# A graph network's second and third layers: sums and splits from GpSimd to VectorE, forms and bias made one group earlier, PSUM pools kept open

## The chip, the cores and the metric

The kernel runs on one core of a Trainium2 chip. The metric is the device time of one execution in microseconds (us). Engines are named as in the profile: PE is TensorE (PEld its weight loads), DVE is VectorE, ACT is ScalarE, POOL is GpSimd, SP is SyncE, which here only issues DMAs.

## The reference

There are 2500 nodes with 256 features and 80000 edges, sorted by destination. After a layer norm with relu come three edge convolutions, and at the end a product with the concatenation of all four states:

```
def _edge_conv(x, src, dst, W, b):
    xi = x[dst]
    xj = x[src]
    m = jnp.concatenate([xi, xj - xi], axis=-1) @ W + b
    s = jax.ops.segment_sum(m, dst, num_segments=N)
    cnt = jax.ops.segment_sum(jnp.ones((dst.shape[0],), m.dtype), dst, num_segments=N)
    return s / jnp.maximum(cnt, 1.0)[:, None]
...
for W, b in ((W0, b0), (W1, b1), (W2, b2)):
    h = jax.nn.relu(_edge_conv(h, src, dst, W, b))
    xs.append(h)
cat = jnp.concatenate(xs, axis=-1)
return cat @ Wf + bf          # out = x + this, with h = relu(layernorm(x)) as input
```

## The kernel before

**What it computes.** The edges become a matrix of counts (how often node n is a source of node m), so a layer is `hT = relu(z summed by counts + hT times (Wa - Wb))` with `z = h Wb / count`. Destinations are cut into five groups of 504, 504, 504, 504 and 486 columns; sources into 20 tiles of 128 nodes, taken two at a time: a *pair of tiles*, number `q` from 0 to 9. `hT` holds the state transposed; `acc` gathers the output.

**Precision by parts.** TensorE's one-pass type fp32r keeps fewer bits than fp32, so every operand is cut in parts. `zh` and `zl` are high and low part of z. `Split(q)` makes three parts of the state of pair q: high (ACT), low (a subtraction), across (one more operation on DVE). `Forms` makes three matching parts of a weight block [Wb | Wf]: high, scaled and last on ACT, two lows and two acrosses on DVE. With both, `times` makes a product from 6 one-pass matmuls per tile; `times_whole` makes it from 2 fp32 matmuls, each of which TensorE runs in two passes (the profile counts both).

**Stages.**

- *Layer 0* builds the counts, group by group: DVE compares keys, PE adds, ACT copies; `finish` writes them to DRAM in bf16 (`a_dram`). `layer(0, g)` multiplies group g meanwhile. During the last group (g = 4) no counts are left to build.
- *Node stage* of layers 1 and 2, for each pair q in `orders[l]`: `Nodes.multiply` (12 one-pass matmuls of 512 columns), `parts` (ACT scales and copies into `tmp` and `zh`, DVE makes `zl` and adds to `acc` twice), `combine` (three subtractions and sums of z into `tmp`), `split` of the pair two places on, `sums` (ACT `sh`, DVE `sl`). Between them `Alone` multiplies the fifth group (8 matmuls of 486 columns per pair); `lone.end` adds its own product and ACT writes `hT`.
- *Stream stage*: groups 0 to 3 are done as two 2x2 block products by a scheme of seven products. There are 2 x 5 chunks; a chunk has seven blocks of counts, cast from bf16 in `staged` to fp32r in `block` (seven buffers, pool `ready`), and each block is used by 4 matmuls of 504 columns. Three blocks are casts on ACT (`b11`, `b21`, `b22`), four are sums on DVE (`r1` to `r4`). `Stream.make` stays five blocks ahead. `tick(n)` puts small jobs between the 70 steps, the splits and forms of the next layer among them.
- *Last layer*: for each pair 12 one-pass matmuls of 256 columns, two additions to `acc`, two output DMAs; splits up to three pairs ahead.

**What sets the order.** Each engine runs its instructions in the order of the Python code (`InOrder` keeps it). Semaphores and the sizes of the pools make them wait. `banks(n, alone)` closes a PSUM pool and opens another; the first tile of a new pool waits for the last users of all tiles of the closed one.

```
def split(q, V=POOLo):
    sp = splits[q] = Split(q)
    sp.high()
    sp.low(V)
    sp.across(DVEo)
...
n.multiply(None if i < whole else splits.pop(q), forms, flat(l))
n.parts()
n.combine(POOLo)
```

All instructions recorded through `InOrder` stand under line L282 in the profile, so one goes by the tiles' names.

Of the kernel before, what the change touches and what calls it, by code (L numbers as in the profile page):

```python
# [313 lines left out]
def by_windows(ctx: ExitStack, tc: tile.TileContext, x, src, dst, Ws, bs, Wf, bf, out, missing):  # L314
# [3 lines left out]
    P = 128  # L318
# [597 lines left out]
    apools.append(first_layer.enter_context(tc.tile_pool(name="apool1", bufs=1)))  # L916
# [8 lines left out]


    LATE = [NT] * 4
    extra = chain(degrees(0), finish(0, a), later_loads(), degrees(1))
    for g in range(NG):
        at = {}  # L930
        own = LATE
        if g + 1 < NG:
            a1 = new_a(g + 1)
            one = build(g + 1, a1)
            left = -(-len([b for b in windows if b[0] == g + 1]) // TURN)
            units = NT + DC * DC
            at = {(i + 1) * (units - 1) // left - 1 for i in range(left)}
            if g:
                own = [u + 1 - i for i, u in enumerate(sorted(at)[1:5])]
        else:  # L940
            extra = shares()
# [19 lines left out]
    banks_of = ctx.enter_context(ExitStack())  # L961

    def banks(n, alone=0):
        nonlocal banks_of
        banks_of.close()
        banks_of = ctx.enter_context(ExitStack())
        ps.append(banks_of.enter_context(tc.tile_pool(name="ps_n", bufs=n, space=PSUM)))
        return banks_of.enter_context(tc.tile_pool(name="ps_alone", bufs=alone, space=PSUM)) if alone else None
# [3 lines left out]
    ready = ctx.enter_context(tc.tile_pool(name="ready", bufs=7))  # L972
# [14 lines left out]
    def combine(to, x, V):  # L987
        V.tensor_sub(to[:, M3:S5 + 1, :], x[:, 1::2, :], x[:, 0:2, :])
        V.tensor_sub(to[:, S2, :], to[:, M3, :], x[:, 3, :])
        V.tensor_add(to[:, M4, :], to[:, S2, :], x[:, 2, :])  # L990
# [3 lines left out]

    E12 = 4096.0
    C1 = 1.0 + 1.0 / E12
    DOWN = 1.0 - 0.5 / E12  # L1000

    class Split:

        def __init__(self, q):
            self.q = q
            t = stage.tile([P, 4 * GS], F32R, name="staged")
            self.parts = [t[:, k * 2 * D:(k + 1) * 2 * D].rearrange("p (c n) -> p c n", c=DC) for k in range(3)]
            self.h = hT[:, :, 2 * q * P:(2 * q + 2) * P]

        def high(self):  # L1010
            ACTo.activation(self.parts[0], self.h, AF.Copy, scale=DOWN)

        def low(self, V):
            V.tensor_sub(self.parts[1], self.h, self.parts[0].bitcast(F32))

        def across(self, V):
            V.scalar_tensor_tensor(self.parts[2], self.parts[1].bitcast(F32), -E12, self.parts[0].bitcast(F32),
                                   op0=OP.mult, op1=OP.add)

    class Forms:  # L1020

        def __init__(self, raw, n, V, rest):
            self.raw, self.n, self.V = raw, n, V
            self.rest = rest
            self.parts = [ready.tile([P, 2, 512], F32R, name="block")[:, :, :n] for _ in range(3)]

        def high(self):
            ACTo.activation(self.parts[0], self.raw, AF.Copy, scale=C1 * DOWN)

        def low(self):  # L1030
            for c in range(DC):
                self.V.scalar_tensor_tensor(self.rest[c], self.raw[:, c, :], C1, self.parts[0][:, c, :].bitcast(F32),
                                            op0=OP.mult, op1=OP.subtract)

        def scaled(self):
            for c in range(DC):
                ACTo.activation(self.parts[1][:, c, :], self.rest[c], AF.Copy, scale=E12)

        def across(self):
            for c in range(DC):  # L1040
                self.V.scalar_tensor_tensor(self.rest[c], self.parts[0][:, c, :].bitcast(F32), -1.0 / E12, self.rest[c],
                                            op0=OP.mult, op1=OP.add)

        def last(self):
            for c in range(DC):
                ACTo.activation(self.parts[2][:, c, :], self.rest[c], AF.Copy, scale=1.0 / C1)

# [5 lines left out]

    def times_whole(to, t, raw):
        for c in range(DC):
            PEo.matmul(to, hT[:, c, t * P:(t + 1) * P], raw[:, c, :], start=(c == 0), stop=(c == DC - 1))
# [4 lines left out]
    class Nodes:  # L1061
# [4 lines left out]
        def multiply(self, split, forms, raw):  # L1066
            self.banks = [bank(), bank()]
            for i, t in enumerate(self.two):
                if split is None:
                    times_whole(self.banks[i], t, raw)  # L1070
                else:
                    times(self.banks[i], split, i, forms)
# [17 lines left out]
        def combine(self, V):  # L1090
            self.raw = tmp()
            combine(self.raw.rearrange("p (s n) -> p s n", s=4), self.zf.rearrange("p (s n) -> p s n", s=4), V)
# [10 lines left out]
    class Pair:  # L1103
# [12 lines left out]
        def make(self, c, what, st, made):  # L1116
            to = made[what] = ready.tile([P, 2, 512], F32R, name="block")[:, :, :GS]
# [27 lines left out]
        def multiply(self, c, part, what, made):  # L1145
            if c == 0:
                self.bank[what] = bank()[:, :GS]
# [40 lines left out]
    class Alone:  # L1188

        def __init__(self, l, order, pool):  # L1190
            self.l, self.order = l, order
            self.c0, self.n = group_of(alone)
            self.to = [pool.tile([P, 512], F32, name="bank")[:, :self.n] for _ in range(DC)]
            self.blocks = {}

        def make(self, p):
            q = self.order[p]
            to = self.blocks[p] = ready.tile([P, 2, 512], F32R, name="block")
# [67 lines left out]
    DVEo.tensor_sub(ws[1][0], ws[1][0], ws[1][1])  # L1266
# [3 lines left out]
    splits = {}  # L1270
    forms = None

    def split(q, V=POOLo):
        sp = splits[q] = Split(q)
        sp.high()
        sp.low(V)
        sp.across(DVEo)

    def flat(l):
        return raws[l].rearrange("p c t d -> p c (t d)") if l < L else wfs[l]  # L1280

    for l in range(1, L):
        order = orders[l]
        whole = 2 if l == 1 else 0
        lone = Alone(l, order, banks(6, 2))
        if l == 1:
            load_alone(0, order)
            split(order[whole])
            forms = Forms(flat(l), 512, DVEo, [tmp(), tmp()])
            forms.high()  # L1290
            forms.low()
            forms.scaled()
            forms.across()
            forms.last()
        pending = []
        stream = Stream(l)
        for i in range(Q + LAG):
            if 0 < i <= Q:
                lone.make(i - 1)
            if i < Q:  # L1300
                q = order[i]
                n = Nodes(l, q)
                n.multiply(None if i < whole else splits.pop(q), forms, flat(l))
# [3 lines left out]
                n.combine(POOLo)  # L1307
# [12 lines left out]
        banks(8)  # L1320
# [6 lines left out]
        coming = []  # L1327

        def tick(n):
            if l == 1 and 2 <= n < 18 and n % 4 == 2:  # L1330
                part = acc[:, (n - 2) // 4 * 5:(n + 2) // 4 * 5, :]
                POOLo.tensor_add(part, part, bf_sb.unsqueeze(1).to_broadcast([P, 5, D]))
            if n == 3:
                combine(wsum, ws[l][0].rearrange("p c (o n) -> p (c o) n", o=2), DVEo)
# [4 lines left out]
            if n == 63:  # L1339
                if l + 1 < L:  # L1340
                    load_alone(0, after)
                else:
                    split(after[3])
            if n == 65:
                split(after[2])
            if n == 64:
                raw = flat(l + 1)
                coming.append(Forms(raw, 512 if l + 1 < L else D, DVEo, [raw[:, c, :] for c in range(DC)]))
                coming[0].high()
                coming[0].low()  # L1350
            if n == 66:
                coming[0].scaled()
# [5 lines left out]
        forms = coming[0]  # L1358

    order = orders[L]  # L1360
    for i, q in enumerate(order):
        po, sp = bank(), splits.pop(q)
        for k in range(2):
            times(po[:, k * D:(k + 1) * D], sp, k, forms)
# [46 lines left out]
```

## Time and profile before

| what | value |
|---|---|
| runs | 495.49, 497.53, 498.29 us; median 497.53 |
| profiled execution: own time | 495.88 us |
| profiled execution: span | 494.0 us |
| granted TensorE clock, mean | 0.99 |
| layer 0 / node 1 / stream 1 | 0-206 / 206-259 / 259-344 us |
| node 2 / stream 2 / last layer | 344-394 / 394-471 / 471-494 us |

The times of all rows are from the start of the span; the own time is 1.9 us longer than the span. In the rows, "x12" merges 12 like instructions, the second number of a timeline row is its length in us, and a bracket at its end says how long the engine was idle before it and what ended that. A matmul's row is longer than the distance to the next one (they overlap), so costs of matmuls are taken from start to start.

### The profile page before, as it was taken

To read this page: it belongs to the slowest core of one execution; us is meant where nothing else is said; L and a number is where in the kernel's file an instruction comes from. 1 tells how busy PE (TensorE), PEld (TensorE's weight loads), DVE (VectorE), ACT (ScalarE), POOL (GpSimd) and SP (SyncE) were. 2 spreads that over 40 slices of the span, in tenths; PEclk is the share of its full clock that TensorE was granted. 3 is DMA by queue.
4 is the path that set the end of the run, shared out by engine and by line. 5 is a ranking of instruction groups with operands and counts; after the bars stand their busy time and mean duration, and the time that the engine had idled before them with its cause. 6 is when DMAs were issued, how large, how long until landed. Compare 5 with 4: busy or idle time off the path is not lost.

```text
span 494.0 us, 7493 instructions
## 1 busy us (share of the span) xinstructions
PE 474.3 (96%) x2728; PEld 367.5 (74%) x2728; DVE 391.7 (79%) x743; ACT 264.6 (54%) x488; POOL 142.9 (29%) x158
## 2 busy tenths in 40 slices
PE   8999999999999999989996999999999999999994
PEld 4888888777777778558865877866788688687684
DVE  8999988888888850168689877997677769689885
ACT  5676677653734340298762444635787644365240
POOL 3682006100101010178786000111787200011252
PEclk9999999999999999999997999999999999999998
DMA  9310098970914509211392541210213944320024
GB/s 285 108 43 1 2 204 152 203 147 0 189 23 92 119 14 197 84 44 42 88 355 72 187 153 49 85 43 0 85 42 101 340 169 137 115 85 1 0 75 141
DMA packets 21847, 52.75 MB, mean 107 GB/s; under 512 B 1977, under 2 KB 12170, under 8 KB 21770
## 3 DMA queue, kind: packets, MB, share of 16 engines
q1 hardware_dynamic: 15018, 34.57, 20.9%
q0 software_dynamic: 5856, 16.51, 17.5%
q10 hardware_dynamic: 928, 1.11, 0.7%
q8 instruction: 23, 0.38, 0.3%
q14 instruction: 22, 0.18, 0.1%
HBM read 36.72 MB, written 16.10 MB: 107 GB/s over the span
## 4 chain that ended last, share of the span: by engine, by line
PE 64%; issue 13%; DVE 11%; POOL 6%; ACT 3%; DMA 2%; SPq 0%; DVEq 0%; POOLq 0%; ACTq 0%
PE bank L282 60%; DVE block L282 5%; PE pz L282 3%; POOL staged L282 2%; POOL acc L282 2%; DMA acc<-in_x_dram 1%; DVE staged L282 1%; DVE tmp L282 1%; POOL tmp L282 1%; DMA staged<-a_dram 1%; DVE st L282 1%; ACT hT L282 1%; POOL ed L282 1%; POOL es L282 0%; ACT block L282 0%
## 5 line engine op out<-in xcount | busy, mean ns | idle before, releaser
L282 ACT CAST block<-staged 128x1008 fp32r<-128x1008 bf16 x80 | 79.3, 1031 | 44.2 <-issue 42.8
L282 POOL TENSOR_TENSOR staged<-hT,staged 128x512 fp32r<-128x512 f32 x28 | 39.9, 1434 | 167.8 <-ACT staged L282 167.8
L282 PE MATMUL bank<-block,zh 128*128 128x504 f32 (+1 forms) x200 | 83.4, 417 | 2.4 <-ACT hT L282 1.3
L282 ACT CAST a<-bank 128x480 fp32r<-128x480 f32 (+1 forms) x105 | 52.9, 565 | 59.3 <-PE bank L282 59.2
L282 PE MATMUL bank<-a,zh 128*128 128x504 f32 (+1 forms) x200 | 84.3, 421 | 0.0
L282 DVE TENSOR_TENSOR one_m<-iota_m,key_m 128x1024 bf16<-128x1024 bf16 (+1 forms) x105 | 72.0, 686 | 14.1 <-PE bank L282 14.0
L282 PE MATMUL bank<-block,zl 128*128 128x504 f32 (+1 forms) x200 | 78.1, 391 | 0.0
L282 PE MATMUL bank<-a,zl 128*128 128x504 f32 (+1 forms) x200 | 77.8, 389 | 0.0
L282 PE MATMUL bank<-block,sh 128*128 128x504 f32 x160 | 69.9, 437 | 4.0 <-DVE block L282 4.0
L282 PE MATMUL bank<-block,staged 128*128 128x512 f32 (+1 forms) x336 | 69.8, 358 | 3.5 <-DVE staged L282 2.1
L282 DVE TENSOR_TENSOR one_n<-iota_n,key_n 128x480 bf16<-128x480 bf16 (+1 forms) x210 | 66.8, 359 | 0.0
L282 PEld LDWEIGHTS bank<-block,staged 128*128 128x128 f32 x336 | 55.1, 188 | 15.5 <-DVE staged L282 3.9
L282 PE MATMUL bank<-block,sl 128*128 128x504 f32 x160 | 63.0, 394 | 0.0
L282 POOL TENSOR_TENSOR tmp<-tmp 128x128 f32<-128x128 f32 (+1 forms) x60 | 46.0, 766 | 31.2 <-ACT tmp L282 24.7
L282 DVE SCALAR_TENSOR_TENSOR staged<-staged 128x512 fp32r<-128x512 f32 x28 | 22.6, 807 | 39.5 <-POOL staged L282 39.5
L282 DVE TENSOR_TENSOR block<-block,staged 128x1008 fp32r<-128x1008 f32 x40 | 52.5, 1313 | 1.4
L282 PEld LDWEIGHTS bank<-block,zh 128*128 128x128 f32 x200 | 38.1, 191 | 14.9 <-ACT hT L282 2.9
L282 POOL DMA_DIRECT2D a_dram<-a x20 | 10.7, 542 | 127.7 <-ACT a L282 127.4
L282 PEld LDWEIGHTS <-one_m 128*128 128x128 bf16 x834 | 39.1, 98 | 9.7 <-issue 3.2
L282 PEld LDWEIGHTS bank<-block,zl 128*128 128x128 f32 x200 | 38.2, 191 | 10.2 <-issue 2.8
L282 PEld LDWEIGHTS bank<-a,zh 128*128 128x128 f32 x200 | 37.8, 189 | 10.7 <-issue 2.6
L282 PEld LDWEIGHTS bank<-a,zl 128*128 128x128 f32 x200 | 37.7, 188 | 9.0 <-issue 2.6
(152 smaller groups left out, 709.2 us busy)
## 6 DMA issues: line engine op xcount, KB each, us to landing
staged<-a_dram SPq DMA_DIRECT2D x52, 504.0 KB, 4.1
a_dram<-a POOLq DMA_DIRECT2D x20, 630.0 KB, 8.9
out_dram<-acc SPq DMA_DIRECT2D x19, 128.0 KB, 2.4
acc<-in_x_dram POOLq DMA_DIRECT2D x3, 640.0 KB, 11.8
wbf<-in_L_gnn_Wf_dram SPq DMA_DIRECT2D x4, 256.0 KB, 7.1
acc<-in_x_dram SPq DMA_DIRECT2D x1, 896.0 KB, 9.4
acc<-in_x_dram ACTq DMA_DIRECT2D x1, 768.0 KB, 6.9
wbf<-in_L_gnn_W_dram SPq DMA_DIRECT2D x3, 256.0 KB
```

What stands on the lines that cost most here:

```text
L282: return self.tc.keep_in_program_order(call(*args, **kwargs))
```

## The change

What it does:

1. `combine` and the low part of each split run on DVE; nothing of layers 1, 2 and the last is left on POOL.
2. `bf` was added to `acc` by POOL in four parts during the first steps of layer 1's stream; it is added by DVE in layer 0's last group.
3. In that group too: `ws[1][0] - ws[1][1]`, the forms of layer 1 and the splits of pairs 0 and 1 (`first_forms`). Their seven blocks take the pool `ready`, which is opened where group 3's counts lay (`second.close()`). So `times_whole` is gone.
4. `r1` and `r2` are added in bf16 inside `staged` (onto `b12` and `b22`) and cast by ACT; `r3` and `r4` stay on DVE and read `staged`. So that sums stay exact, counts are cut at 85 before the check that all edges were found.
5. PSUM is divided once, into `ps_two` and `ps_six`, for all stages behind layer 0. `Alone` uses the two, `Nodes` and the last layer the six, the stream all eight in turn. No pool is closed any more.

```diff
+        DVEo.tensor_scalar(deg, deg, float(256 // 3), None, op0=OP.min)
         DVEo.reduce_sum(found, deg.rearrange("p i c -> p (i c)"), axis=mybir.AxisListType.X)
...
+    class Split:
+        def __init__(self, q, parts):
+            h = hT[:, :, 2 * q * P:(2 * q + 2) * P]
+            high, low, across = self.parts = [p.rearrange("p (c n) -> p c n", c=DC) for p in parts]
+            ACTo.activation(high, h, AF.Copy, scale=DOWN)
+            DVEo.tensor_sub(low, h, high.bitcast(F32))
+            DVEo.scalar_tensor_tensor(across, low.bitcast(F32), -E12, high.bitcast(F32), op0=OP.mult, op1=OP.add)
+            splits[q] = self
...
+    def first_forms():
+        DVEo.tensor_sub(ws[1][0], ws[1][0], ws[1][1])
+        yield
+        coming.append(Forms(flat(1), [flat(1)[:, c, :] for c in range(DC)]))
+        coming[0].high()
+        coming[0].low()
+        yield
+        coming[0].across()
+        coming[0].last()
+        yield
+        for q in range(2):
+            two = [block().rearrange("p c n -> p (c n)") for _ in range(2)]
+            Split(q, [two[0][:, :2 * D], two[0][:, 2 * D:], two[1][:, :2 * D]])
+            yield
+        for t in range(0, NT, 5):
+            DVEo.tensor_add(acc[:, t:t + 5, :], acc[:, t:t + 5, :], bf_sb.unsqueeze(1).to_broadcast([P, 5, D]))
+            yield
...
         else:
-            extra = shares()
+            second.close()
+            ready = ctx.enter_context(tc.tile_pool(name="ready", bufs=7, side="right"))
+            extra = chain(shares(), first_forms())
...
-    def banks(n, alone=0):
-        nonlocal banks_of
-        banks_of.close()
...
+    ps_two = ctx.enter_context(tc.tile_pool(name="ps_two", bufs=2, space=PSUM))
+    ps_six = ctx.enter_context(tc.tile_pool(name="ps_six", bufs=6, space=PSUM))
+    def any_bank():
+        turn_of[0] += 1
+        return (ps_six if (turn_of[0] - 1) % 8 < 6 else ps_two).tile([P, 512], F32, name="bank")
...
             elif what == "r1":
-                DVEo.tensor_add(to, b11, b12)
+                DVEo.tensor_add(b12, b11, b12)
+                ACTo.copy(to, b12)
             elif what == "r2":
-                DVEo.tensor_add(to, made["r1"].bitcast(F32), b22)
+                DVEo.tensor_add(b22, b12, b22)
+                ACTo.copy(to, b22)
             elif what == "r3":
-                DVEo.tensor_sub(to, b11, made["r2"].bitcast(F32))
+                DVEo.tensor_sub(to, b11, b22)
             else:
-                DVEo.tensor_add(to, made["r2"].bitcast(F32), b21)
+                DVEo.tensor_add(to, b22, b21)
...
-                n.multiply(None if i < whole else splits.pop(q), forms, flat(l))
+                n.multiply(splits.pop(q), coming[0])
-                n.combine(POOLo)
+                n.combine()
...
-            if l == 1 and 2 <= n < 18 and n % 4 == 2:
-                part = acc[:, (n - 2) // 4 * 5:(n + 2) // 4 * 5, :]
-                POOLo.tensor_add(part, part, bf_sb.unsqueeze(1).to_broadcast([P, 5, D]))
```

How it moves instructions, at three places.

*End of layer 0, start of layer 1.* The first rows are DVE's of the changed kernel in the last group: `wt` and `wbf` are layer 1's weights (the forms work in place in `wbf`), `block` the buffers of `ready`.

```order
L282 TENSOR_TENSOR wt<-wt,wbf 128x512
L282 SCALAR_TENSOR_TENSOR wbf<-wbf,block 128x512 x2
L282 SCALAR_TENSOR_TENSOR wbf<-block,wbf 128x512 x2
L282 TENSOR_TENSOR block<-hT,block 128x512
L282 SCALAR_TENSOR_TENSOR block<-block 128x512
L282 TENSOR_TENSOR block<-hT,block 128x512
L282 SCALAR_TENSOR_TENSOR block<-block 128x512
L282 TENSOR_TENSOR acc<-acc,bf_sb 128x1280 x4
```

Behind the first row, all of them stood later or elsewhere: the forms and the first split at the start of layer 1, the additions of `bf` on POOL. On PE, from the last group's own product (`hT,wt`) on:

```order
 L282 MATMUL bank<-a,zl 128x486
 L282 MATMUL bank<-hT,wt 128x486 x4
-L282 MATMUL bank<-wbf,hT 128x512 x8
+L282 MATMUL bank<-block 128x512 x24
 L282 MATMUL bank<-block,staged 128x512 x12
 L282 MATMUL bank<-block,zh 128x486
```

Eight fp32 matmuls became 24 one-pass ones, whose operands lie in `block` alone.

*Node stage of layer 1, DVE, one pair* (`tmp` are z and its combinations, `staged` a split's parts):

```order
 L282 SCALAR_TENSOR_TENSOR acc<-bank,share,acc 128x256 x2
+L282 TENSOR_TENSOR tmp<-tmp 128x256
+L282 TENSOR_TENSOR tmp<-tmp 128x128 x2
+L282 TENSOR_TENSOR staged<-hT,staged 128x512
 L282 SCALAR_TENSOR_TENSOR staged<-staged 128x512
 L282 TENSOR_TENSOR sl<-tmp,sh 128x512
 L282 TENSOR_TENSOR zl<-tmp,zh 128x2x256
 L282 SCALAR_TENSOR_TENSOR acc<-bank,share,acc 128x256 x2
```

Four instructions per pair came to DVE, between the additions to `acc` and the split's last part.

*Stream stage of layer 1, DVE, first chunk* (`staged` are counts in bf16 here, `wsum` sums of weights made at step 3):

```order
-L282 TENSOR_TENSOR block<-staged 128x2x504
-L282 TENSOR_TENSOR block<-block,staged 128x2x504
-L282 TENSOR_TENSOR block<-staged,block 128x2x504
-L282 TENSOR_TENSOR block<-block,staged 128x2x504
+L282 TENSOR_TENSOR staged<-staged 128x2x504 x2
+L282 TENSOR_TENSOR block<-staged 128x2x504 x2
 L282 TENSOR_TENSOR wsum<-wt 128x256
 L282 TENSOR_TENSOR wsum<-wsum,wt 128x128 x2
```

Two of DVE's four results per chunk go to `staged`, and ACT, with three casts per chunk before, has five.

More of the change, by code (lines that the diff above doesn't have):

```diff
@@ L1020, in by_windows @@
[L1020 to L1046, printed above, removed]
@@ L1064, in __init__, with multiply @@
             self.l, self.q, self.two = l, q, (2 * q, 2 * q + 1)
-        def multiply(self, split, forms, raw):
+        def multiply(self, split, forms):
             self.banks = [bank(), bank()]
[L1068 to L1072, printed above, removed]
+            for i in range(2):
+                times(self.banks[i], split, i, forms)
         def parts(self):
@@ L1116, in make @@
         def make(self, c, what, st, made):
[L1117 removed]
+            to = made[what] = block()[:, :, :GS]
             b11, b21, b12, b22 = (st[:, g, h::2, :] for g in range(2) for h in range(2))
@@ L1269, in by_windows, with split @@
     orders = [None, list(range(Q)), [8, 9, 0, 1, 2, 3, 7, 6, 5, 4], [8, 9, 0, 1, 2, 3, 7, 6, 5, 4]]
[L1270 to L1280, printed above, removed]
+    def split(q):
+        tile_ = stage.tile([P, 4 * GS], F32R, name="staged")
+        Split(q, [tile_[:, k * 2 * D:(k + 1) * 2 * D] for k in range(3)])
     for l in range(1, L):
         order = orders[l]
-        whole = 2 if l == 1 else 0
-        lone = Alone(l, order, banks(6, 2))
+        lone = Alone(l, order)
         if l == 1:
             load_alone(0, order)
[L1288 to L1294, printed above, removed]
+            split(order[2])
         pending = []
@@ L1338, in tick @@
                 split(after[(n - 49) // 7])
[L1339 to L1345, printed above, removed]
+            if n == 63 and l + 1 < L:
+                load_alone(0, after)
+            if n in ((65,) if l + 1 < L else (63, 65)):
+                split(after[2 + (65 - n) // 2])
             if n == 64:
                 raw = flat(l + 1)
-                coming.append(Forms(raw, 512 if l + 1 < L else D, DVEo, [raw[:, c, :] for c in range(DC)]))
+                coming[:] = [Forms(raw, [raw[:, c, :] for c in range(DC)])]
                 coming[0].high()
```

87 lines of the change are left out of this document (45 added, 42 removed).

## The prediction

> **What bounds the kernel now.** I read the engines' totals first, then busy time by stage, then the rows on both sides of each gap on PE.
>
> ```profile
> PE 474.3 (96%) x2728; PEld 367.5 (74%) x2728; DVE 391.7 (79%) x743; ACT 264.6 (54%) x488; POOL 142.9 (29%) x158
> ```
>
> ```profile
> core 0: us, PE busy (x) PEld busy (x) DVE busy (x) ACT busy (x) POOL busy (x), PEclk, DMA share, GB/s
> 186.00:204.00 18.00, 18.00 (x79) 14.56 (x78) 0.53 (x1) 0.00 (x0) 0.00 (x0) 1.00 0.68 133
> 206.00:258.90 52.90, 50.92 (x200) 37.48 (x200) 38.54 (x54) 39.98 (x67) 39.73 (x40) 1.00 0.37 123
> 258.90:343.60 84.70, 79.34 (x308) 59.11 (x309) 75.65 (x75) 37.32 (x44) 12.83 (x6) 0.96 0.26 88
> 268.10:274.70 6.60, 6.60 (x20) 5.33 (x21) 6.32 (x8) 1.49 (x2) 0.00 (x0) 0.65 0.47 156
> 343.60:394.00 50.40, 49.31 (x209) 39.00 (x209) 35.33 (x53) 37.33 (x62) 32.25 (x37) 1.00 0.41 138
> 394.00:471.00 77.00, 76.47 (x308) 57.81 (x309) 62.60 (x69) 35.51 (x43) 5.52 (x4) 1.00 0.24 82
> 471.00:494.00 23.00, 15.81 (x121) 14.55 (x120) 15.91 (x30) 5.55 (x8) 9.32 (x6) 0.94 0.35 116
> ```
>
> PE bounds it: 96% of the span. Only work taken from PE, gaps on PE, and lost clock can bring time. The stages show where that lies. The two streams issue the same 308 matmuls, yet stream 1 takes 84.7 us and stream 2 77.0: 7.7 us to find there. The last layer has PE busy 15.8 of 23.0. Node 1 has 2.0 of idle, node 2 1.1. In the last group (186 to 204) DVE, ACT and POOL are empty.
>
> **A: `bf` leaves stream 1.** These are POOL's additions, two of the block sums that DVE makes meanwhile, and PE:
>
> ```profile
> 252.48 14.41 POOL L282 TENSOR_TENSOR acc<-acc,bf_sb 128x1280 f32<-128x1280 f32 x4
> ```
>
> ```profile
> 264.24 3.72 DVE L282 TENSOR_TENSOR block<-staged,block 128x1008 fp32r<-128x1008 bf16 x1
> 267.88 1.19 DVE L282 TENSOR_TENSOR block<-block,staged 128x1008 fp32r<-128x1008 f32 x1
> ```
>
> ```profile
> 262.47 0.39 PE L282 MATMUL bank<-block,sl 128*128 128x504 f32 x1
> 264.19 0.50 PE L282 MATMUL bank<-block,sh 128*128 128x504 f32 x1 [1.33 <-DVE block L282]
> 264.76 0.39 PE L282 MATMUL bank<-block,sh 128*128 128x504 f32 x1
> 264.99 0.39 PE L282 MATMUL bank<-block,sl 128*128 128x504 f32 x1
> 268.01 0.79 PE L282 MATMUL bank<-block,sh 128*128 128x504 f32 x1 [2.63 <-DVE block L282]
> ```
>
> Beside POOL's addition a block sum takes 3.72 us; the moment POOL ends (252.48 + 14.41 = 266.89) the next takes 1.19. One matmul should follow the last after 0.23 (264.76 to 264.99). The two waits cost 264.19 - 262.47 - 0.23 = 1.49 and 268.01 - 264.99 - 0.23 = 2.79. Behind the second, the clock is 0.65 for 6.6 us: 6.6 x 0.35 = 2.31. Together **-6.6**. In the last group the four additions cost DVE some 1.19 x 1280/1008 = 1.5 each, 6 us with PE busy on counts; with what B adds there it is 11.5 of 18 empty us. Were that cover gone, DVE would bring the excess over 18 to 206.00.
>
> A page bears on the 2.31. The Trainium skill, "TensorE: Matmul & The Clock Gate", Part 1: The HAM clock gate, has the clock fall only behind an idle window of about 3.4 us. By it a gap of 2.63 would not be the cause, the loss could stay, and the sum below would be 2.3 smaller. The rows speak against it: the clock is 1.00 in the stage before and 0.65 right behind this gap. I let the rows decide.
>
> **B: one pass for the first two pairs.**
>
> ```profile
> 206.00 7.13 PE L282 MATMUL bank<-wbf,hT 128*128 128x512 f32 x16 [0.67 <-ACT hT L282]
> 212.57 3.35 PE L282 MATMUL bank<-block,staged 128*128 128x512 f32 x12
> ```
>
> ```profile
> 368.10 2.96 PE L282 MATMUL bank<-block,staged 128*128 128x512 f32 x12
> 370.90 0.38 PE L282 MATMUL bank<-block,zh 128*128 128x486 f32 x1
> ```
>
> Sixteen passes took 212.57 - 206.00 = 6.57. Twelve one-pass matmuls take 2.80, 24 take 5.60: **-1.0**. The wait of 0.67 ahead (ACT writes `hT`) stays. Forms and splits of DVE and ACT, some 8 x 0.69 on DVE, go into the last group.
>
> **C: wait for the split of pair 2.**
>
> ```profile
> 217.53 0.40 PE L282 MATMUL bank<-block,staged 128*128 128x512 f32 x1
> 218.51 0.51 PE L282 MATMUL bank<-block,staged 128*128 128x512 f32 x1 [0.59 <-POOL staged L282]
> 219.76 2.59 PE L282 MATMUL bank<-block,staged 128*128 128x512 f32 x10 [0.74 <-DVE staged L282]
> ```
>
> 219.76 - 217.53 - 2 x 0.23 = 1.77 goes: the split no longer stands behind the forms. Next late is pair 3's split, queued on DVE behind two pairs' first work; I give it 0.3 (0, if DVE is early, to 1.25, the last distance above). **-1.5**.
>
> **D and F: PSUM kept open.**
>
> ```profile
> 254.83 3.42 PE L282 MATMUL bank<-hT,wt 128*128 128x486 f32 x8
> 258.92 0.50 PE L282 MATMUL bank<-block,zh 128*128 128x504 f32 x1 [0.67 <-ACT hT L282]
> ```
>
> ```profile
> 342.37 0.39 PE L282 MATMUL bank<-block,zl 128*128 128x504 f32 x1
> 343.62 2.57 PE L282 MATMUL bank<-block,staged 128*128 128x512 f32 x10 [0.87 <-ACT hT L282]
> ```
>
> The stream's first matmul waited for ACT's `hT` only because the pools were closed, and so did layer 2's first node matmul. D: of 0.67 plus some 0.2 in slower neighbours I leave 0.2 for the cast that stands behind `hT` on ACT; -0.7 in each layer, **-1.4** (0 to -1.8). F: 343.62 - 342.37 - 0.23 = 1.02, **-1.0** (0, if the forms on DVE and ACT are as late, to -1.0).
>
> **E: two sums in bfloat16.** One late block in each stream:
>
> ```profile
> 328.35 0.39 PE L282 MATMUL bank<-block,sl 128*128 128x504 f32 x1
> 329.28 0.50 PE L282 MATMUL bank<-block,zh 128*128 128x504 f32 x1 [0.54 <-DVE block L282]
> ```
>
> 329.28 - 328.35 - 0.23 = 0.70, and 0.2 in neighbours at 0.33 instead of 0.23: 0.9; the other stream has the same near 457. DVE needs 4 x 1.2 = 4.8 of the 28 x 0.23 = 6.4 us of a chunk, and the jobs of `tick` make it late. The additions in bf16 aren't in the trace. Bounds are a bf16 comparison of 1024 elements and the 1.19 of above:
>
> ```profile
> L282 DVE TENSOR_TENSOR one_m<-iota_m,key_m 128x1024 bf16<-128x1024 bf16 (+1 forms) x105 | 72.0, 686 | 14.1 <-PE bank L282 14.0
> ```
>
> ```profile
> L282 ACT CAST block<-staged 128x1008 fp32r<-128x1008 bf16 x80 | 79.3, 1031 | 44.2 <-issue 42.8
> ```
>
> I take 0.69, the nearer by type: 3.8 per chunk. ACT goes from 3 casts to 5, 5.2 of 6.4, so a bias or relu there can be late by one; with five blocks of lead I count nothing. **-1.8** (0 to -1.8).
>
> **G: node stages on DVE alone.** What each instruction costs without POOL beside it:
>
> ```profile
> 269.00 0.41 DVE L282 TENSOR_TENSOR wsum<-wt 128x256 f32<-128x256 f32 x1
> 269.45 0.62 DVE L282 TENSOR_TENSOR wsum<-wsum,wt 128x128 f32<-128x128 f32 x2
> ```
>
> ```profile
> 366.33 0.69 DVE L282 SCALAR_TENSOR_TENSOR staged<-staged 128x512 fp32r<-128x512 f32 x1 [0.82 <-POOL staged L282]
> 366.94 0.68 DVE L282 TENSOR_TENSOR sl<-tmp,sh 128x512 fp32r<-128x512 f32 x1
> ```
>
> ```profile
> 479.62 0.86 DVE L282 SCALAR_TENSOR_TENSOR acc<-bank,share,acc 128x256 f32<-128x256 f32 x2
> 480.40 0.99 DVE L282 SCALAR_TENSOR_TENSOR staged<-staged 128x512 fp32r<-128x512 f32 x1
> 481.32 0.86 DVE L282 SCALAR_TENSOR_TENSOR acc<-bank,share,acc 128x256 f32<-128x256 f32 x2
> ```
>
> From start to start: 512 columns 0.61, two additions to `acc` 0.78, combine 0.45 + 0.54 = 0.99. Per pair `zl`, `sl`, across and low (4 x 0.61, and 0.2 for the low's two-part view, an estimate) + 0.78 + 0.99 = **4.4 us**. PE's pair is 12 x 0.233 + 8 x 0.233 x 486/512 = 4.57. It fits, by 0.15. A split has two pairs of lead, so single delays are absorbed. What remains of node 2's idle through POOL's split (some 0.4) goes: **-0.4**.
>
> **H: last layer.** DVE per pair now: 481.32 - 479.62 = 1.70, with POOL making the low beside it. After: 0.78 + 0.79 + 0.61 = 2.18, against 12 matmuls of 256 columns that run ahead and wait. Six splits are made here, of which the first are ahead; 0.48 x 6 = 2.9, less the waits that POOL's chain (low, then across) causes today, some 1.9 (an estimate). **+1.0** (0 to +2.9).
>
> **Sum:** -6.6 - 1.0 - 1.5 - 1.4 - 1.0 - 1.8 - 0.4 + 1.0 = -12.7. The profiled execution took 495.88 us (span 494.0 and 1.9 around it): 483.2. It lies 1.65 below the median of 497.53; by the median 484.8. I say 485.
>
> **Rivals.** *DVE bounds the node stages.* With 4.4 of 4.57 it needs little: waits for ACT between `zh` and `zl`, or for PE's banks, of 0.5 per pair make it 4.9. The first four pairs live off the lead; 16 x 0.35 = 5.6: 490.5. For it speaks the thin margin, against it that half of DVE's inputs are a pair old. 0.18.
>
> *DVE's stretched times aren't POOL's doing* (the other side). In the node stages `zl` took 0.94 on average, beside POOL, ACT and PE alike:
>
> ```profile
> L282 DVE TENSOR_TENSOR zl<-tmp,zh 128x512 fp32r<-128x512 f32 x20 | 18.8, 941 | 11.0 <-ACT zh L282 10.7
> ```
>
> If ACT's or PE's traffic made that 0.94/0.68, a ratio of 1.38, DVE's pair is 4.4 x 1.38 = 6.1, 1.5 over PE's: 16 x 1.5 = 24, 509. It turns slower than before where 16 pairs eat 12.7, at 4.57 + 0.8 = 5.4 per pair. Against it: the 0.69 and 0.68 of 366.33 stand in the same stage with ACT and PE busy. 0.05.
>
> *The clock falls in the last layer.* PE was busy two thirds of the time there, at 0.94. Should it fall to half, a pair of 12 matmuls takes 2 x 1.4 = 2.8 instead of DVE's 2.18: 10 x 0.6 = 6, 491. 0.05.
>
> *bfloat16 sums as slow as the others:* 1.19 each, E gives nothing, 486.6. 0.10.
>
> *The clock loss of A stays,* at another gap early in stream 1: 2.3 more, 487. 0.08. By the page's rule above it would stay too.
>
> *It does nothing,* where DVE's sums are late for another reason than POOL: 4.3 of A and the clock stay, and H and DVE's load eat the rest; 495 to 498. 0.03, since 3.72 turning to 1.19 at POOL's end is plain.
>
> **How the numbers follow.** My forecast, 482 to 487 within the sizes of D to H, has 0.51. With the late bf16 sums and the kept clock loss it is 0.69, all below 488. The range takes in half the DVE-bound case, and below the sum the case that H costs nothing and neighbours of the waits go too (-3 to -5): 480 to 491. Runs of this kernel differ by 0.5%, 2.5 us, which is about what a measurement can tell from no change. Faster: 0.51 + 0.10 + 0.08 + 0.18 + 0.05 = 0.92. Same 0.03, slower 0.05.
>
> **What would show it.** A: no DVE block sum over 1.3 us in the first chunk, clock 1.00 through stream 1, and that stream at 77 to 78 us like stream 2. B: the first two pairs in 5.6. C: no wait over 0.5 near 12 us into layer 1. D, F: no `hT` as releaser at the streams' start or layer 2's. E: bf16 sums near 0.69, no DVE block as releaser late in a stream. G: PE's pair stays 4.57; waits for `staged` from DVE that grow from pair to pair mean the first rival. H: a last layer of 24 us. Wrong I'd be above all with `zl`, `sl` and low still at 0.9 and POOL empty.

## The result, and the profile after

The changed kernel takes 484.34 us (median of 4 runs, 483.3 to 485.88), beside it the kernel before 497.91 us (495.49 to 499.07): ratio 0.9736, 95% interval 0.969 to 0.9783. The forecast was 485.0, in 480 to 491. The profiled execution has a span of 481.5 us, the sum of the prediction 481.3 (483.2 less 1.9).

The same two views, of the kernel after. The lines of the second are the stages, each from its first matmul on PE to that of the next; the first of them is the end of layer 0.

```profile
PE 469.0 (97%) x2736; PEld 367.8 (76%) x2736; DVE 387.5 (80%) x840; ACT 303.5 (63%) x530; POOL 43.2 (9%) x66
```

```profile
core 0: us, PE busy (x) PEld busy (x) DVE busy (x) ACT busy (x) POOL busy (x), PEclk, DMA share, GB/s
190.00:206.20 16.20, 15.53 (x64) 11.67 (x63) 8.28 (x8) 2.42 (x6) 0.00 (x0) 1.00 0.63 145
206.20:254.95 48.75, 48.73 (x208) 38.94 (x209) 41.11 (x88) 35.69 (x60) 0.00 (x0) 1.00 0.38 125
254.95:331.36 76.41, 76.41 (x311) 57.84 (x309) 57.67 (x76) 56.27 (x65) 0.00 (x0) 1.00 0.31 103
331.36:380.92 49.56, 49.00 (x209) 38.84 (x208) 40.32 (x87) 37.09 (x61) 0.00 (x0) 1.00 0.40 129
380.92:457.32 76.40, 76.40 (x310) 57.83 (x309) 57.01 (x77) 55.38 (x65) 0.00 (x0) 1.00 0.27 90
457.32:481.40 24.08, 15.95 (x121) 14.78 (x119) 16.72 (x34) 5.66 (x8) 0.00 (x0) 0.93 0.33 110
```

PE now has no idle to speak of in node 1 and both streams, and POOL does nothing. Stage by stage, from first matmul to first matmul:

| stage | before, us | after, us | difference |
|---|---|---|---|
| layer 0 | 206.00 | 206.20 | +0.2 |
| node 1 | 52.92 | 48.75 | -4.2 |
| stream 1 | 84.70 | 76.41 | -8.3 |
| node 2 | 50.34 | 49.56 | -0.8 |
| stream 2 | 77.09 | 76.40 | -0.7 |
| last layer, to the last matmul | 16.42 | 17.04 | +0.6 |
| behind the last matmul | 6.51 | 7.10 | +0.6 |

What PE waited for behind layer 0, from the view of waits: total, how often, the longest. First the kernel before, then after.

```profile
engine line waited for: us in total, times, longest us
PE bank L282 <- DVE block L282: 5.0, 4, 2.6
PE bank L282 <- ACT hT L282: 2.9, 4, 0.9
PE bank L282 <- DVE staged L282: 2.1, 3, 0.9
PE bank L282 <- POOL staged L282: 0.6, 1, 0.6
```

```profile
PE bank L282 <- DVE staged L282: 1.9, 6, 0.3
PE bank L282 <- ACT hT L282: 0.7, 1, 0.7
```

Of 10.6 us of waits 2.6 are left. The waits for a block of counts are gone, one of four for `hT` is left, at layer 1's start, and six short ones for a split's parts: two in layer 2, 11 us behind its start, and four in the last layer.

Layer 1's start on PE, and one pair of it on DVE:

```profile
206.20 5.76 PE L282 MATMUL bank<-block 128*128 128x512 f32 x24 [0.67 <-ACT hT L282]
211.81 2.96 PE L282 MATMUL bank<-block,staged 128*128 128x512 f32 x12
```

```profile
217.47 0.69 DVE L282 TENSOR_TENSOR zl<-tmp,zh 128x512 fp32r<-128x512 f32 x1
218.08 0.87 DVE L282 SCALAR_TENSOR_TENSOR acc<-bank,share,acc 128x256 f32<-128x256 f32 x2
218.87 1.06 DVE L282 TENSOR_TENSOR tmp<-tmp 128x256 f32<-128x256 f32 x3
219.85 0.68 DVE L282 TENSOR_TENSOR staged<-hT,staged 128x512 fp32r<-128x512 f32 x1
220.56 0.69 DVE L282 SCALAR_TENSOR_TENSOR staged<-staged 128x512 fp32r<-128x512 f32 x1
221.17 0.68 DVE L282 TENSOR_TENSOR sl<-tmp,sh 128x512 fp32r<-128x512 f32 x1
221.78 0.69 DVE L282 TENSOR_TENSOR zl<-tmp,zh 128x512 fp32r<-128x512 f32 x1
```

The first two pairs take 5.61 us. DVE's pair is 221.78 - 217.47 = 4.31 us without a gap; the prediction had 4.4 against PE's 4.57. `zl` takes 0.69 where it took 0.94. The new sums in bf16 and the additions of `bf` (in the last group of layer 0, from 193.39 on):

```profile
L282 DVE TENSOR_TENSOR staged<-staged 128x1008 bf16<-128x1008 bf16 x40 | 27.1, 678 | 20.8 <-ACT block L282 20.4
L282 DVE TENSOR_TENSOR acc<-acc,bf_sb 128x1280 f32<-128x1280 f32 x4 | 5.7, 1483 | 0.0
```

In the last layer DVE has become the bound:

```profile
466.86 1.77 PE L282 MATMUL bank<-block,staged 128*128 128x256 f32 x12 [0.34 <-DVE staged L282]
468.97 1.77 PE L282 MATMUL bank<-block,staged 128*128 128x256 f32 x12 [0.34 <-DVE staged L282]
```

A pair takes 468.97 - 466.86 = 2.11 us there, DVE's two additions and one split (forecast 2.18). The clock of 0.93 in the last line of the stages is not PE's loss: it is 1.00 up to 477.9, and PE's last matmul starts at 474.36.

### The profile page after: what moved, and what is told of

It reads as the page before. It is cut to its first block, busy times and chain, and to the rows that moved or that the text cites. A ratio compares the mean times of both kernels' runs of the same rounds, so it can differ in the third digit from the quotient of the medians.

```text
span 481.5 us, 7530 instructions
## 1 busy us (share of the span) xinstructions
PE 469.0 (97%) x2736; PEld 367.8 (76%) x2736; DVE 387.5 (80%) x840; ACT 303.5 (63%) x530; POOL 43.2 (9%) x66
## 4 chain that ended last, share of the span: by engine, by line
PE 88%; DVE 6%; POOL 3%; ACT 1%; issue 1%; DVEq 0%; ACTq 0%; POOLq 0%
PE bank L282 84%; PE pz L282 4%; DVE staged L282 2%; DVE acc L282 2%; POOL acc L282 2%; POOL ed L282 1%; DVE zl L282 1%; POOL es L282 1%; DVE tmp L282 0%; DVE st L282 0%; PE turned L282 0%; ACT zh L282 0%; ACT hT L282 0%; ACT junk L282 0%; DVE mv L282 0%
## 5 line engine op out<-in xcount | busy, mean ns | idle before, releaser
L282 ACT CAST block<-staged 128x1008 fp32r<-128x1008 bf16 x120 | 117.9, 1031 | 16.7 <-DVE staged L282 6.3
L282 DVE TENSOR_TENSOR block<-staged 128x1008 fp32r<-128x1008 bf16 x40 | 46.9, 1204 | 5.3 <-PE bank L282 3.9
L282 PEld LDWEIGHTS bank<-block,zh 128*128 128x128 f32 x200 | 37.6, 188 | 10.4 <-issue 2.5
L282 PE MATMUL bank<-one_n,one_m 128*128 128x120 bf16 x834 | 44.2, 208 | 0.4 <-DVE one_n L282 0.4
L282 DVE TENSOR_TENSOR staged<-staged 128x1008 bf16<-128x1008 bf16 x40 | 27.1, 678 | 20.8 <-ACT block L282 20.4
L282 PE MATMUL pz<-wbf,hT 128*128 128x256 f32 x160 | 38.4, 385 | 0.1
L282 PEld LDWEIGHTS bank<-block,sh 128*128 128x128 f32 x160 | 30.1, 188 | 10.4 <-issue 3.5
```

The costliest lines, as they stand in the source:

```text
L282: return self.tc.keep_in_program_order(call(*args, **kwargs))
```

## The experiments

Single executions differ by up to 1.5 us in layer 0 (205.84 to 207.33 in these runs) and by up to 3 behind the last matmul (5.9 to 8.95), which most of the experiments leave as they are. The stages between repeat far better: where an edit does not touch them, to 0.02. So where a part is small, the stages' own lengths (from first matmul to first matmul) are compared with those of the table above, and the medians beside them. The edits are shown shortened.

**`bf` on DVE in the last group, alone.** The kernel before, with only this part of the change:

```
-            extra = shares()
+            extra = chain(shares(), add_bf())     # four tensor_adds on DVE
...
-            if l == 1 and 2 <= n < 18 and n % 4 == 2:
-                POOLo.tensor_add(part, part, bf_sb ...)
```

> The kernel before, with one thing changed: bf is added by DVE in layer 0's last group. Theory (POOL beside DVE stretches DVE's block sums, the late sums stop PE, the stop lowers the clock): all of term A goes, 6.6 us, so about 491; no block sum over 1.4 us in stream 1, granted clock 1.00 through that stream, everything behind as before. Rival 1 (the clock falls there for another reason): 4.3 us, 493.3, and 6 us at 0.65 stay. Rival 2 (the sums are late whoever adds bf): 497.

489.04 us against 496.34, ratio 0.9857 (0.9806 to 0.9908). Stream 1 takes 336.89 - 258.77 = 78.12 us instead of 84.70: 6.58 less, and its clock is whole:

```profile
258.90:338.00 79.10, 77.70 (x313) 58.50 (x314) 65.52 (x71) 38.15 (x44) 4.86 (x3) 1.00 0.27 92
```

```profile
PE bank L282 <- ACT hT L282: 2.9, 4, 0.9
PE bank L282 <- DVE staged L282: 2.1, 3, 0.9
PE bank L282 <- DVE block L282: 1.1, 2, 0.5
PE bank L282 <- POOL staged L282: 0.6, 1, 0.6
```

Only the waits for `block` changed, from 5.0 to 1.1. Both rivals fall. One detail missed: a block sum of stream 1 still takes 2.12 us (at 308.46), where none over 1.4 was expected. It stands beside POOL's low part of a split (307.96 to 309.51).

**`bf` back in stream 1, by POOL and by DVE.** The changed kernel, with the four additions at the old steps of `tick`, on either engine.

> The changed kernel, with bf added by POOL in the first steps of stream 1 as before. Theory (any DVE operation on two SBUF operands is stretched beside POOL's addition, the bf16 sums too): the waits come back, 4 to 6.6 us, 488 to 491, and with a wait over 2 us the clock falls. Rival (bf16 sums keep 0.7 us, only r3 and r4 are stretched to 3.7): 8.8 us of DVE in a chunk of 6.4 with a lead of 4.6 is absorbed, 484 to 485.

> The changed kernel, with bf added at the same steps of stream 1, but by DVE. Theory (the harm came from POOL's engine, not from the place): 5.7 us more on DVE over 18 steps (16 us), where it has 2.6 us to spare in each 6.4; late by less than the lead, 484 to 485. Rival (the place is what counts, the early stream has no lead yet): waits of 2 us and more for block, 487 to 489.

DVE: 484.56, ratio to the kernel before 0.9758 (0.9714 to 0.9802), and PE's waits are those of the changed kernel. The place costs little: stream 1 takes 77.43 instead of 76.41, 1.0 more, since some blocks come just in time and matmuls follow at 0.33 to 0.37 instead of 0.23, which no wait of the view shows. POOL: 492.84, ratio 0.9922 (0.9897 to 0.9947), 8.5 us more than the changed kernel, above the 4 to 6.6 expected. I had the place wrong: POOL's queue is empty now, so each addition ran as soon as DVE had finished its five tiles of `acc`, all four inside the node stage. There the cause shows at its plainest. These are POOL's second addition, DVE's row beside it, and PE's rows behind the first addition:

```profile
230.90 3.06 POOL L282 TENSOR_TENSOR acc<-acc,bf_sb 128x1280 f32<-128x1280 f32 x1 [9.17 <-DVE acc L282]
```

```profile
230.73 3.71 DVE L282 TENSOR_TENSOR tmp<-tmp 128x256 f32<-128x256 f32 x3
```

```profile
223.32 0.49 PE L282 MATMUL bank<-block,staged 128*128 128x512 f32 x1 [1.58 <-DVE staged L282]
224.05 4.09 PE L282 MATMUL bank<-block,staged 128*128 128x512 f32 x10 [0.23 <-DVE staged L282]
```

Three combine operations that take 1.06 take 3.71, and end 0.5 us behind POOL's instruction (234.44 and 233.96): DVE stands while POOL runs. Four such stops, of some 2.6 us each, stand in a stage where DVE has 0.25 us to spare per pair, and node 1 takes 56.37 us instead of 48.75: 7.6 us more for 10.4 of standing, a half clock behind the first wait (last section) among them. The Trainium skill, "SBUF — State Buffer", Who interferes with whom, has an instruction of VectorE with two SBUF inputs and a GpSimd instruction that reads SBUF exclude each other for the whole instruction. The rows agree: 3.71 instead of 1.06.

**Needless work on DVE in the node stages.** After `combine`, its first operation once more, or all three:

```
+            DVEo.tensor_sub(r4[:, M3:S5 + 1, :], z4[:, 1::2, :], z4[:, 0:2, :])    # 0.45 us
```

> The changed kernel, with the first of the three combine operations done twice in each pair of the node stages (0.45 us more on DVE). Theory (DVE's pair takes 4.31, PE's 4.56, and nothing else in these stages is near): 4.76, 0.2 over PE's in 18 pairs, less what the lead absorbs: +2 to 3.5 us, about 487. Rival (DVE still has slack that the rows don't show): 484 to 485. Rival 2 (waits between ACT and DVE add up as soon as DVE is full): +6 and more.

> The changed kernel, with all three combine operations done twice (0.99 us more on DVE per pair). Theory: 5.3 against 4.56, 0.74 in 18 pairs, less a lead of 1 to 2 us in each stage: +10 to 13 us, 495 to 497, so the change would have brought nothing at that DVE time. Rival (slack): +5 or less. Rival 2 (waits add up): +15 or more.

487.21 us and 498.02 us; ratios to the kernel before 0.9797 (0.9758 to 0.9836) and 1.002 (0.9998 to 1.0043). The two node stages grow by 1.46 + 1.16 = 2.6 us and by 7.33 + 6.37 = 13.7 us. With 0.99 more, DVE's pair is 5.30 long and PE follows it:

```profile
224.40 2.61 PE L282 MATMUL bank<-block,staged 128*128 128x512 f32 x10 [0.22 <-DVE staged L282]
229.69 2.60 PE L282 MATMUL bank<-block,staged 128*128 128x512 f32 x10 [0.23 <-DVE staged L282]
```

From 224.40 to 229.69 are 5.29 us. So DVE's margin in these stages is what its rows say, 0.25 us per pair, and at 1 us more per pair the whole change would have brought nothing. The second came out 0.7 above the 10 to 13 that I expected: 18 pairs of 0.74 are 13.3 already, so nothing of the 1 to 2 us of lead that I allowed per stage is seen.

**r1 and r2 in fp32 again.**

```
-                DVEo.tensor_add(b12, b11, b12)
-                ACTo.copy(to, b12)
+                DVEo.tensor_add(to, b11, b12)       # r2, r3, r4 likewise
```

> The changed kernel, with r1 and r2 made in fp32 by DVE into block as before (four sums on DVE, three casts on ACT). Theory (term E): one late block in each stream, 0.9 us each: +1.8, about 486. Rival 1 (bf16 in place brought nothing, the late blocks of before came from the splits' waits for POOL): 484 to 484.5. Rival 2 (with the combines gone to DVE the stream starts later too): +3 or more.

485.95 us, ratio 0.9786 (0.9742 to 0.983). Each stream has its late block back and is 0.59 us longer (77.00 and 76.99):

```profile
317.90 0.39 PE L282 MATMUL bank<-block,sl 128*128 128x504 f32 x1
318.65 0.50 PE L282 MATMUL bank<-block,zh 128*128 128x504 f32 x1 [0.36 <-DVE block L282]
```

**PSUM pools closed again at each stage.**

```
-        turn_of[0] = 0
+        banks(8)                # and banks(6, 2) ahead of each node stage
```

> The changed kernel, with the PSUM pools closed and opened at each stage as before (6 and 2, then 8). Theory (terms D and F): +0.7 at each stream's start, with ACT's hT as releaser, and +1.0 at the start of layer 2: +2.4, about 487; the last layer's start may wait too, another 0.5 to 1. Rival (closing costs nothing, the first wait is for ACT's cast or the forms anyway): 484 to 485.

486.34 us, ratio 0.9795 (0.975 to 0.984). The old waits are there, three more for `hT`:

```profile
256.21 0.50 PE L282 MATMUL bank<-block,zh 128*128 128x504 f32 x1 [0.67 <-ACT hT L282]
...
333.31 0.48 PE L282 MATMUL bank<-block,staged 128*128 128x512 f32 x1 [0.87 <-ACT hT L282]
```

The stages from node 1 to stream 2 take 1.21, 0.69, 1.28 and -0.33 us more, 2.85 together. In the changed kernel the first matmul of a stream has no wait but the second comes 0.37 late; with closed pools that 0.37 is inside the wait, which is why stream 2 is shorter.

**First two pairs in fp32, forms at layer 1's start.**

```
-                n.multiply(splits.pop(q), coming[0])
+                n.multiply(None if l == 1 and i < 2 else splits.pop(q), flat(l))
```

> The changed kernel, with the first two pairs of layer 1 multiplied in fp32 (16 passes instead of 24 one-pass matmuls) and layer 1's forms made at that layer's start, as before; bf still on DVE in the last group. Theory (terms B and C): +1.0 for the passes and +1.5 for the wait for pair 2's split behind the forms: +2.5, about 487. Rival (C came from POOL's low alone, which is gone here too): +1.0 and a wait of at most 0.6, 485.5.

485.60 us, ratio 0.9774 (0.973 to 0.9817); node 1 takes 2.13 us more. The passes:

```profile
206.41 7.13 PE L282 MATMUL bank<-wbf,hT 128*128 128x512 f32 x16 [0.67 <-ACT hT L282]
212.97 3.36 PE L282 MATMUL bank<-block,staged 128*128 128x512 f32 x12
...
218.62 0.50 PE L282 MATMUL bank<-block,staged 128*128 128x512 f32 x1 [0.30 <-DVE staged L282]
219.35 1.90 PE L282 MATMUL bank<-block,staged 128*128 128x512 f32 x7 [0.23 <-DVE staged L282]
```

212.97 - 206.41 = 6.56, 0.95 more than 5.61; the other 1.2 are the late split and its neighbours. The two waits shown cost 0.46 and 0.49 from start to start. The median is nearer the rival's 485.5, and no wait is over 0.6, as it has it; but node 1 grew by twice its +1.0. Both hold in part. The twelve matmuls of the pair with the waits (from 217.93) take 3.86 us here, 3.10 in the changed kernel (from 216.36) and 4.66 in the kernel before (from 217.53). So the forms alone bring back 0.76 of the 1.56.

**combine and the splits' low on POOL again.**

```
-            DVEo.tensor_sub(low, h, high.bitcast(F32))
+            V.tensor_sub(low, h, high.bitcast(F32))        # V = POOLo but for the first two splits
...
-            combine(self.raw..., self.zf...)
+            combine(self.raw..., self.zf..., POOLo)
```

> The changed kernel, with combine and the splits' low part on POOL again (from pair 2 of layer 1 on). Theory (terms G and H): the node stages lose 0.2 to 0.5 us each to late splits, the last layer gains 1.0, since POOL works beside DVE there: 483.8 to 484.5. Rival 1 (DVE stands still while POOL runs, as in the run where POOL added bf, where three sums of 1.07 took 3.7): DVE's pair goes over PE's 4.57 in the node stages, +0.3 to 1 per pair, 488 or more. Rival 2 (POOL is the better place for all of it): 482.5 or less.

484.89 us, ratio 0.9763 (0.9719 to 0.9807): not told from the changed kernel's 0.9736. Inside it differs. The streams are 0.45 and 0.43 us longer (POOL's low makes one block late again), node 1 0.25 longer, node 2 0.47 shorter, the last layer 0.68 shorter. PE's waits:

```profile
PE bank L282 <- DVE staged L282: 1.5, 3, 0.9
PE bank L282 <- ACT hT L282: 0.7, 1, 0.7
PE bank L282 <- DVE block L282: 0.3, 2, 0.2
```

So the first part of the change, the one with the most instructions, is a wash: what the streams and node 1 gain, node 2 and the last layer give back. Rival 1 of this run is not seen, though POOL does stop DVE. In node 1 of this run `zl` takes 0.93 on average, `sl` 0.83 and across 0.76, instead of 0.69, 0.68 and 0.69: 0.45 us of standing per pair. But combine and low, 1.7 us per pair, are no longer DVE's, and its busy time in node 1 falls from 41.1 to 31.6 us.

**One wait on PE at a time.** The changed kernel, with subtractions on DVE at five steps that do nothing but delay it.

```
+            for i in range({7: 8, 21: 10, 42: 12}.get(n, 0) if l == 1 else {7: 14, 21: 16}.get(n, 0)):
+                DVEo.tensor_sub(scrap, acc[:, 0:2, :], acc[:, 2:4, :])
```

> The changed kernel, with 8, 10, 12, 14 and 16 needless subtractions of 512 columns (0.61 us each) put on DVE at five steps of the two streams, so that PE waits once at each for about 0.5, 1.5, 2.7, 4 and 5 us, with no other wait near. Theory (one wait of 2.6 us is enough to lower the clock): full clock behind the two shorter waits, half clock for some 6 us behind the three longer. Rival 1 (it takes over 3.4 us of idle, as the Trainium skill, TensorE: Matmul & The Clock Gate, Part 1: The HAM clock gate, has it): half clock only behind the last two. Rival 2 (before, it took both waits of stream 1 together): no fixed length. Time about 484 + 14 + 2 to 3 per fall of the clock, 502 to 508.

522.46 us in one run, against the 502 to 508 expected. The waits came out longer than planned, 3.26, 3.15, 5.31, 7.61 and 7.51 us, so that the short ones are missing, and the clock fell at all five. That speaks against rival 1, since 3.15 and 3.26 are under its 3.4; but the some 6 us of the theory are not seen behind these two either. The first, with windows of 2 us around it (the clock is the number behind POOL's):

```profile
270.76 0.49 PE L282 MATMUL bank<-block,zh 128*128 128x504 f32 x1 [3.26 <-DVE block L282]
```

```profile
270.00:272.00 2.00, 1.24 (x4) 1.01 (x5) 1.90 (x3) 0.59 (x1) 0.00 (x0) 0.81 0.28 26
272.00:274.00 2.00, 2.00 (x7) 1.55 (x6) 1.90 (x3) 1.37 (x2) 0.00 (x0) 0.50 0.81 306
274.00:276.00 2.00, 2.00 (x9) 1.67 (x8) 1.93 (x4) 1.62 (x2) 0.00 (x0) 0.84 0.78 230
```

The short wait that was missing is in the run with `bf` on POOL: behind 1.58 us at 223.32 the clock is

```profile
223.30:225.00 1.70, 1.44 (x3) 1.02 (x4) 1.70 (x3) 0.95 (x2) 0.00 (x0) 0.70 0.00 0
225.00:227.00 2.00, 2.00 (x6) 1.54 (x5) 1.93 (x7) 0.47 (x1) 0.00 (x0) 0.50 0.00 0
```

**Last six pairs in fp32, and splits ahead of combine.** The experiments left two places where PE waits for DVE. The first edit takes the splits out of the last layer, the second puts each node-stage split ahead of combine:

```
+            if q in splits:
+                times(to, splits[q], k, coming[0])
+            else:                                   # fp32, from hT and the weights themselves
+                PEo.matmul(to, hT[:, c, ...], flat(L)[:, c, :], ...)
...
-        for k in order[i + 1:i + 4]:
-            if k not in splits:
-                split(k)
```

```
-                n.combine()
                 if i + AHEAD_H < Q and order[i + AHEAD_H] not in splits:
                     split(order[i + AHEAD_H])
+                n.combine()
```

> The changed kernel, with the last six pairs of the last layer multiplied in fp32 from the state itself (8 passes of 256 columns instead of 12 one-pass matmuls), so that no split is made in that layer; the last layer's forms take their low part in the bias rows, which are free by then, and leave the weights as they are. Theory (DVE bounds the last layer at 2.11 us per pair): PE's pair is 8 x 0.205 = 1.64, DVE's 0.78, so 6 x 0.4 = 2.4 less at the end of PE, and the output's DMAs follow: -2 to -2.8, about 482. Rival 1 (the end is set by the output DMAs, two issues of 0.7 per pair on one queue): -0.5 or less. Rival 2 (fp32 passes cost more beside the one-pass ones, or the clock falls): 0 or above.

> As the run with the last six pairs in fp32, and in the node stages the split of the pair two places on stands ahead of combine on DVE instead of behind it. Theory: the two waits for staged at the start of layer 2 (0.48 and 0.49) go, since that split is made 0.99 us earlier, and nothing waits for combine that soon: another -1.0, about 481. Rival (the wait moves to zl or to the sums): within 0.3 of the run without it.

481.75 us with the first, ratio 0.9694 (0.9668 to 0.9721), and 479.59 us with both, ratio 0.9657 (0.9628 to 0.9686). Only the second interval lies below the changed kernel's (0.969 to 0.9783). A last-layer pair in fp32 takes 8 x 0.216 = 1.73 us instead of 2.11, and the layer to its last matmul 15.86 instead of 17.04: 1.2 less, half of what I expected: a pass takes 0.216, not 0.205, and only four of the last six pairs had waited for DVE. The second edit takes node 2 from 49.56 to 48.56, the 1.0 expected, and node 1 from 48.76 to 48.52. The medians moved further, by 2.6 and 2.2; the stages do not show where the rest lies. What PE waits for then, behind layer 0:

```profile
PE bank L282 <- ACT hT L282: 0.7, 1, 0.7
```

## Why the prediction was right, point by point

- **A (-6.6).** Shown: 6.58 in stream 1 with that edit alone. The engine counts far more than the place: on DVE in the same steps the additions cost stream 1 1.0 us. The rival that the block sums are late for another reason is excluded by the same two runs.
- **The half clock, 2.31 of A.** It went with the waits: 1.00 in stream 1 of the run with that edit alone. The sum by the rows held, not the one that was 2.3 smaller.
- **B (-1.0)** is 0.95. **C (-1.5)** is 1.56 from kernel to kernel, 4.66 less 3.10 us for the twelve matmuls. The 0.3 that I gave for pair 3's just-in-time split is in the 3.10: twelve take 2.80 elsewhere. It shows as no wait, only as matmuls that follow more slowly. But the split that is late is that of pair 3, not of pair 2, and the forms are only half of the reason. With them alone put back the group takes 0.76 more; with combine and low alone on POOL 0.24 (219.84 - 216.50 = 3.34); in the kernel before, with both, 1.56. There POOL makes the low only at 217.18, behind two combines. The group before is 0.39 faster too (3.19 to 2.80), which I had not counted.
- **D and F (-2.4)** are 2.85: F 1.03 as forecast, D 0.9 per layer, at the bound of its range. I left 0.2 for the cast behind `hT`, which costs the second matmul, not the first.
- **E (-1.8)** was mis-sized: 1.2, as the undoing of r1 and r2 shows. The price of a sum was right (0.678 against 0.69). Wrong was to count all of the late block as the sums' own: POOL's low made the block late as well, and low and combine on DVE brought another 0.9. Stage by stage the parts add up. Of stream 1, 1.71 us are left when A is taken off; undone alone, the pools give 0.69, the sums 0.59, combine and low 0.45: 1.73. In stream 2 it is -0.33 + 0.59 + 0.43 = 0.69, of 0.69.
- **G (-0.4) and H (+1.0)** were to cost 0.6 together. G had the wrong sign: combine and low on DVE bring 0.25 in node 1 and cost 0.47 in node 2. H is +0.7, and its step was right, 2.11 against 2.18 per pair. Together they cost 0.9, which the 0.9 in the streams, not foreseen under G, pays back. The medians cannot tell this: 0.55 apart.
- **The sum.** Undone one by one the parts come to 6.58 + 2.13 + 2.85 + 1.18 - 0.02 = 12.72 by the stages, which lost 13.31 in all; the other 0.6 is in node 1, where forms and POOL together cost pair 3 more than each alone. The two profiles differ by 494.0 - 481.5 = 12.5, since layer 0 and the stretch behind the last matmul took 0.2 and 0.6 more, within what they differ by anyway. So 481.3 against 481.5 is partly luck: C, D and the streams brought more than I had forecast, G and those two ends less.
- **The rivals.** DVE did not bound the node stages, but by 0.25 us per pair only. The other side had its threshold at 5.4 us per pair; the run at 5.30 has ratio 1.002. It did not come, because the stretch was POOL's: without POOL `zl` takes 0.69 in the same stage, beside the same ACT and PE, and with combine and low on POOL again 0.93. The clock did not fall in the last layer while PE worked. I had misread the 0.94 of the kernel before: there too it is 1.00 until 491.1, and the last matmul starts at 487.47.

## What to carry to other kernels

Work on GpSimd isn't free for VectorE: while a GpSimd instruction read SBUF here, VectorE's two-input instructions stood still, so look for VectorE rows of several times their usual length and for a GpSimd row that ends where they end. Before moving such work onto VectorE, add up one period of that engine without the stretched rows and compare it with the period of the engine that bounds; here 4.31 against 4.56 us was enough, and 5.30 would have given everything back. Moving such work is not a gain in itself either: combine and low stopped DVE for 0.45 us per pair from POOL and cost it 1.7 of its own, and moving them brought nothing on the whole. And where two changes relieve the same late instruction, undo each alone before one of them gets the credit: in the streams they simply added up, at pair 3 of node 1 together they had cost more than the sum.

## What the hardware showed that I had not expected

The clock of TensorE falls behind shorter waits than I had thought. It fell to half behind single waits of 1.58, 2.30 (PE's row at 352.00 of the run with 0.99 more on DVE), 3.15, 3.26, 5.31, 7.51 and 7.61 us, and in the kernel before during one of 2.63 that followed one of 1.33; behind single waits of 1.08 (`bf` on POOL) and 1.15 us (0.99 more on DVE) it stayed whole. For 1.58 and 3.26 it fell only some 0.6 and 0.5 us after PE had started again.

How long the half clock lasts goes in steps. Behind 3.26, by the three windows above, it is (0.19 + 0.50 + 0.16) x 2 us x 2 = 3.4 us. The like sums give 3.4 behind 1.58, 2.30 and 3.15 too, 6.8 for 1.33 with 2.63, for 5.31 and for 7.51, and 10.2 for 7.61, part of it inside the wait. From one change of the clock to the next, the trace of the run with single waits has 3.41, 13.65, 3.41, 27.31, 6.83, 88.75, 10.24, 13.65 and 6.83 us, all whole multiples of 3.41. So the clock changes at the edges of fixed windows. The Trainium skill, "TensorE: Matmul & The Clock Gate", Part 1: The HAM clock gate, counts in free-running windows of about 3.4 us, which agrees with that step, and has the clock fall after at least one idle window. Read as 3.4 us without a matmul, that does not agree: 1.58 was enough.

What the traces fit is a window in which PE is idle for about half. In the window that ends with the fall PE was busy for 1.69 of 3.41 us with the wait of 1.58 (220.55 to 223.96) and for 0.95 with that of 2.30 (349.25 to 352.66); windows with 2.03 (the wait of 1.15) and 2.17 (1.08) left the clock whole. Behind the last matmul one with 1.81 let it fall and one with 1.75 did not, so the border is not sharper than that. In the kernel before the window from 262.42 to 265.83, with 1.64, holds the wait of 1.33 and the first 0.45 of the second: the fall took both waits, and the rest of the second kept the next window at half. Whether a wait of 1.3 to 1.6 us does harm should then depend on where in a window it falls; no run moved one wait across an edge.
